# One PSUM ring for every use, and another order of the first pair's work, in a two-layer graph attention kernel

## The chip, the cores and the metric

The kernel runs on one core of a Trainium2 chip. The metric is device time in microseconds (us) of the whole launch. Lower is better. The engines are named as in the profile: PE is TensorE (PEld is its weight load), DVE is VectorE, ACT is ScalarE, POOL is GpSimd, and SP issues most DMAs.

## The reference, cut to what matters

Sixty-four graphs of 256 nodes with 512 features pass through two layers that share one 0/1 adjacency matrix:

```python
# layer 0: attention with 8 heads of 64, masked by adj
q, k, v = x @ Wq + bq, x @ Wk + bk, x @ Wv + bv
scores = q @ k.T / 8 + (1 - adj) * -1e9
x = layernorm(x + softmax(scores) @ v @ Wo + bo)
# layer 1: graph convolution
x = layernorm(x + (adj @ x) @ weight + bias)
```

All inputs and outputs are float32.

## The kernel before, in words

**Digits.** A plain float32 product is slow on PE, so most products are done in three products of float32r "digits". Each operand is cut into a high part, a low part and their scaled difference. The product then runs the three digit pairs (1, 0, 2) into one PSUM tile. Cutting one 128x512 operand costs ACT one or two operations and DVE two. For x it is `x_high` on ACT and `x_rest` on DVE (L262, L263). For a block of queries or keys, `product` first copies PSUM to a tile `uncut` on ACT (L329). Then `qk_high` (ACT, L334) and `qk_rest` (DVE, L341 and L343 or L345) cut it, and keys need a last scaling by ACT, `k_low` (L350). For weights it is `split_high` (ACT, L122) and `split_rest` (DVE L127, L128, then ACT L129).

**Weights.** Each of five weight sets (`v`, `qk0`, `qk1`, `o`, `l`) is cut once, in the ring tiles `wr` (six tiles, three to a set, so two sets at a time), and is kept in HBM by three 1 MB DMAs that SP issues (`keep`, L134). Later uses are loaded from there by POOL (`load_w`, L114) in the order of the list `STAGES`.

**Pairs.** Graphs are worked on two at a time: 32 pairs, `p` = 0 to 31. Heads come in two groups `g` = 0 and 1 of four heads. One pair's steps are: products of queries and keys of group 0, `scores(p, 0)`, the values' four blocks (`v`), queries and keys of group 1 (blocks 2 and 3), `values(p, 0)`, `scores(p, 1)`, and `values(p, 1)`, then the output product `o`, a layernorm, `adj_x`, the product `l` and a layernorm. `first(w)` and `second(w)` interleave the pair `w` with its neighbours w - 1 and w + 1. `start()` does the first pair and `last()` the last.

**Order.** On PE, DVE and ACT the instructions stand in the order in which the code lists them (`manual_schedule`). An engine that waits holds up everything listed after it on that engine. In `last()` that holds for PE alone. SP and POOL follow the scheduler's order.

**scores.** `scores(p, g)` (L393) makes eight PSUM tiles in four chunks of two. A chunk is 12 matmuls of 64x128 by 64x256. Two row halves of the array write two different tiles, and three digits of two heads go into each. ACT then takes the exponential of each tile into `e` (L409), DVE multiplies by the mask (`masked`, L414) and adds (`summed`, L419).

**values.** `values(p, g)` (L354) uses three tiles: the sums of the exponentials (L362, copied by ACT at L364), and one tile for each graph (L372, copied to `vc` by ACT at L376). DVE divides and writes `O` (L379 to L391).

**PSUM.** The eight banks are split into two rings. `ps_at` has five, for `scores` and `values`. `ps_mm` has three, for every `product`, `adj_x` (L491) and the transposes. A new tile takes the bank that was released longest ago in its ring, and its first matmul waits until the readers of that bank's last tile are done.

**The first pair.** Its weights are cut while it runs. Its first queries and keys (group 0) come from plain float32 products (`operands` returns one pair of operands) and are then cut into digits for `scores(0, 0)`. Its order in `start()` is: q, k of group 0; two `v` blocks; `scores(0, 0)`; two more `v` blocks; q, k of group 1; `values(0, 0)`; `scores(0, 1)`; then q, k of pair 1. The digits of `wo` are cut in `first(1)`, and those of the second layer's weight in `second(1)`, through their arguments `more[0]`, `more[1]` and `more[2]`.

Of the kernel before, what the change touches and what calls it, by code (L numbers as in the profile page):

```python
# [8 lines left out]
F32 = mybir.dt.float32  # L9
F32R = mybir.dt.float32r  # L10
I32 = mybir.dt.int32
AF = mybir.ActivationFunctionType
# [23 lines left out]
def fast(tc, x, adj, wq, bq, wk, bk, wv, bv, wo, bo, w1, b1, out):  # L36
# [27 lines left out]
    wring = pool("wr", 6)  # L64
    scratch = pool("scratch", 1, space=bass.MemoryType.DRAM)
    small = pool("small", 2)
    ps_at = pool("ps_at", 5, space=bass.MemoryType.PSUM)
    ps_mm = pool("ps_mm", 3, space=bass.MemoryType.PSUM)

    XC, XF, XP, R, Q, K, V, E, SM, O, SET, HL, ST, LN = ({} for _ in range(14))  # L70
    RAW, SCRATCH, W, UNCUT = {}, {}, {}, {}
# [25 lines left out]

    STAGES = [("v", 0), ("qk1", 0), ("qk0", 1)]  # L100
    for p in range(1, NP):
        STAGES += [("v", p), ("qk1", p), ("o", p - 1), *([("qk0", p + 1)] if p + 1 < NP else []), ("l", p - 1)]
    STAGES += [("o", NP - 1), ("l", NP - 1)]
# [99 lines left out]
    acc = cpool.tile([P, 2, N // 32], F32, name="acc")  # L203

    def adj_t():
        pt = ps_mm.tile([P, NC, N], F32, name="mm")
# [14 lines left out]
    def bv_wo():  # L221

        wide = one.tile([P, DC, P], F32, name="z")
        nc.vector.tensor_copy(wide, bv_s[:, :, None].to_broadcast([P, DC, P]))
        pm = ps_mm.tile([P, D], F32, name="mm")
        for d in range(DC):
            nc.tensor.matmul(pm, wide[:, d, :], RAW["o", d], start=d == 0, stop=d == DC - 1)
        nc.vector.tensor_tensor(bo_s, bo_s, pm, op=OP.add)
# [3 lines left out]
    def x_first(i):  # L232
        if i == 0:
            for d in range(DC):
                if d % 2 == 0:
                    t = one.tile([P, 2, D], F32, name=f"e{2 + d // 2}")
                XF[0, d] = t[:, d % 2]
        pt = ps_mm.tile([P, DC, P], F32, name="mm")
# [65 lines left out]
        return [pairs[i] for i in (1, 0, 2)]  # L304

    def product(name, p, j):
        pm = ps_mm.tile([P, D], F32, name="mm")
        pairs = [operands(name, p, j, k) for k in range(DC)]
        n = len(pairs[0])
        for i in range(n):  # L310
            for k in range(DC):
                nc.tensor.matmul(pm, *pairs[k][i], start=i == 0 and k == 0, stop=i == n - 1 and k == DC - 1)  # L312
        scale = RHO if n == 3 else 1.0
        b, c = divmod(j, 2)
        if name in "ol":
            r = R[p][b][:, c]
            if c == 0:
                ST[p, name, b] = two.tile([P, 2], F32, name="sums")
            nc.vector.scalar_tensor_tensor(r, pm, scale, r, op0=OP.mult, op1=OP.add, accum_out=ST[p, name, b][:, c:c + 1])  # L319
        elif name == "v":  # L320
            if c == 0:
                V[p, b] = two.tile([P, NC, D], F32, name="v")
            nc.scalar.activation(V[p, b][:, c], pm, AF.Copy, scale=scale)
        else:
            T, bias = (K, bk_s) if name == "k" else (Q, bq_s)
            if c == 0:
                T[p, b] = one.tile([P, 2, 3, D], F32R, name=name + "T")
            UNCUT[name, p, j] = two.tile([P, D], F32, name="uncut")
            nc.scalar.activation(UNCUT[name, p, j], pm, AF.Identity, bias=bias[:, j:j + 1], scale=scale)  # L329

    def qk_high(name, p, j):
        if 0 <= p < NP:
# [21 lines left out]
    def values(p, g, between=([], [])):  # L354
        if not 0 <= p < NP:
            do(*between)
            return
        at = ps_at.tile([P, 2, N], F32, name="at")
        for b in range(2):
            sm = SM.pop((p, g, b))  # L360
            for h in range(4):
# [2 lines left out]
        nc.scalar.activation(zc, at, AF.Copy)  # L364
        vc = []
        for b in range(2):
            at = ps_at.tile([P, 2, N], F32, name="at")
# [25 lines left out]
    def scores(p, g):  # L393
        if not 0 <= p < NP:
            return
        for b in range(2):
            for kc in range(NC):

                sc = [ps_at.tile([P, 2, N], F32, name="at") for s in range(2)]
                keys = slice(b * N + kc * P, b * N + (kc + 1) * P)  # L400
                for a in range(2):
                    for i in (1, 0, 2):
                        for s in range(2):
                            r = slice(s * HD, (s + 1) * HD)
                            nc.tensor.matmul(sc[s][:, a, :], K[p, g][r, a, i, keys], Q[p, g][r, a, i, b * N:(b + 1) * N],  # L405
                                             start=i == 1, stop=i == 2)
                e = E[p, g, b, kc] = one.tile([P, 2, 2, N], F32, name=f"e{2 * b + kc}")
                for s in range(2):
                    nc.scalar.activation(e[:, s], sc[s], AF.Exp, scale=RHO * qscale)  # L409

    def masked(p, g, b, kc):
        if 0 <= p < NP:
# [70 lines left out]
    def adj_x(p, b, half):  # L483

        if 0 <= p < NP:
            t = HL.pop((p, b, half))
            pm = ps_mm.tile([P, 2, N], F32, name="mm")
            for j in range(2):
                for mc in range(NC):
                    for i in range(2):  # L490
# [20 lines left out]
    def first(w, more=([], [], [])):  # L511
# [41 lines left out]

    def start():
        do(*((x_first, i) for i in range(4)), *((x_high, 0, i) for i in range(4)))
        v, qk1, qk0 = (pairs_of(ring_high, ring_rest, *stage) for stage in STAGES[:3])
# [17 lines left out]
        do((bv_wo,), (x_rest, 1, 2), (x_rest, 1, 3), (block, "q", 1, 0), masks(0, 1, 0), qk0[:2],  # L574
           (block, "k", 1, 0), qk0[2:4], (k_low, 1, 0), masks(0, 1, 1),
           (block, "q", 1, 1), qk0[4:6], (o_high, 0, 0, 0), (o_rest, 0, 0, 0),
           (block, "k", 1, 1), qk0[6:], (k_low, 1, 1), (stage_end, 0), (o_high, 0, 1, 0), (o_rest, 0, 1, 0))

    def last():

# [45 lines left out]
    count = ps_mm.tile([P, 1], F32, name="mm")  # L626
# [182 lines left out]
```

## Time and profile before

| what | us |
|---|---|
| median of 3 runs (2483.57 to 2483.84) | 2483.81 |
| the profiled execution, whole | 2484.97 |
| its span in the trace | 2483.2 |
| PE, PEld busy in the span | 2429.8, 1932.3 |
| DVE, ACT, POOL busy | 2012.2, 1506.9, 438.8 |
| one pair in the steady part (1209.65 to 1284.58 in the trace) | 74.93 |

The trace is of one execution. Times in it count from the start of its span, which is 1.77 us shorter than the same execution's whole time. PE's busy time is modelled from the instructions' sizes, so a PE that is shown busy may still wait a little between two matmuls. A bracket in a line of the timeline gives the idle time just before the group and what ended it.

### The profile page before, as it was taken

The numbers are of one execution on the slowest core, as the hardware profiler recorded it, in microseconds if no ns is written. First come the engines' busy times: TensorE is split into PE (matmuls) and PEld (weight loads), VectorE is DVE, ScalarE is ACT, GpSimd is POOL, SyncE is SP. The second block draws the span as 40 slices with busy tenths as digits, with TensorE's granted clock in tenths as the row PEclk, the third lists the DMA queues.
The fourth block names the chain that finished last, engine by engine and source line by source line (L and its number), as shares of the span: only waits on it lengthen the run. The fifth ranks groups of instructions, "written<-read, shape, count | busy, mean of one in ns | idle before, by whom it ended". The sixth has DMA issues, their size and how long they took to land.

```text
span 2483.2 us, 42881 instructions
## 1 busy us (share of the span) xinstructions
PE 2429.8 (98%) x16910; PEld 1932.3 (78%) x16910; DVE 2012.2 (81%) x3319; ACT 1506.9 (61%) x2802; POOL 438.8 (18%) x720
## 2 busy tenths in 40 slices
PE   8879999999999999999999999999999999999997
PEld 5657787787887787877887877877877877877876
DVE  6777889787889788888888888788888888888866
ACT  5556566666566566566565566566566666566554
POOL 0001111112111112112112112112122121122110
PEclk9989999999999999999999999999999999999998
DMA  7568877778777788777779777779778788778650
GB/s 244 176 212 271 273 238 227 266 250 272 259 239 235 258 252 285 250 237 239 255 248 299 248 226 247 248 253 303 240 224 256 249 255 290 239 226 267 243 187 36
DMA packets 370719, 603.45 MB, mean 243 GB/s; under 512 B 272848, under 2 KB 275152, under 8 KB 310224
## 3 DMA queue, kind: packets, MB, share of 16 engines
q0 software_dynamic: 65664, 478.18, 52.4%
q1 hardware_dynamic: 302736, 120.37, 21.2%
q8 instruction: 135, 2.21, 0.4%
q10 hardware_dynamic: 2112, 2.10, 0.2%
q14 instruction: 72, 0.59, 0.1%
HBM read 551.29 MB, written 49.28 MB: 242 GB/s over the span
## 4 chain that ended last, share of the span: by engine, by line
PE 90%; DVE 2%; ACT 1%; DMA 1%; issue 0%; POOL 0%; POOLq 0%; DVEq 0%; ACTq 0%; SPq 0%
PE mm L312 67%; PE at L405 9%; PE at L372 8%; PE mm L491 5%; PE at L362 2%; DMA r<-in_x_dram 0%; ACT r L464 0%; ACT waste L447 0%; DVE sl L262 0%; DVE wr L128 0%; DVE sd L263 0%; DVE e L414 0%; DVE r L428 0%; DVE r L319 0%; DVE hl L481 0%
## 5 line engine op out<-in xcount | busy, mean ns | idle before, releaser
L414 DVE TENSOR_TENSOR e<-e,adjT 128x1024 f32<-128x1024 f32 x256 | 304.7, 1222 | 1.2 <-ACT e L409 1.2
L312 PE MATMUL mm<-wr,sl 128*128 128x512 f32 x1024 | 279.5, 394 | 12.0 <-ACT wr L129 8.0
L312 PE MATMUL mm<-wr,sh 128*128 128x512 f32 x1024 | 276.3, 391 | 0.0
L312 PE MATMUL mm<-wr,sd 128*128 128x512 f32 x1024 | 275.2, 390 | 0.0
L312 PE MATMUL mm<-low,wr 128*128 128x512 f32 x992 | 273.0, 396 | 1.7 <-DVE low L262 1.7
L312 PE MATMUL mm<-high,wr 128*128 128x512 f32 x992 | 267.6, 391 | 0.0
L312 PE MATMUL mm<-diff,wr 128*128 128x512 f32 x992 | 265.9, 390 | 0.0
L409 ACT ACTIVATE e<-at 128x512 f32<-128x512 f32 x512 | 257.3, 627 | 8.7 <-PE at L405 8.5
L447 ACT ACTIVATE waste<-r,ln 128x512 bf16<-128x512 f32 x256 | 183.9, 718 | 110.8 <-DVE ln L440 108.7
L405 PEld LDWEIGHTS at<-qT,kT 64*128 64x128 f32 x3072 | 204.8, 188 | 57.9 <-issue 25.5
L405 PE MATMUL at<-qT,kT 64*128 64x256 f32 x3072 | 238.1, 294 | 11.5 <-ACT kT L350 7.3
L312 PEld LDWEIGHTS mm<-wr,sl 128*128 128x128 f32 x1024 | 191.0, 189 | 53.7 <-ACT wr L129 10.0
L372 PE MATMUL at<-e,v 128*32 128x256 f32 x4096 | 232.7, 379 | 0.0
L341 DVE SCALAR_TENSOR_TENSOR qT<-qT,uncut 128x512 fp32r<-128x512 f32 x128 | 87.9, 687 | 171.7 <-ACT qT L334 171.7
L464 ACT ACTIVATE r<-r,ln 128x512 f32<-128x512 f32 x256 | 194.1, 807 | 52.5 <-DMA x<-in_x_dram 27.1
L312 PEld LDWEIGHTS mm<-wr,sh 128*128 128x128 f32 x1024 | 193.8, 189 | 41.1
L453 POOL TENSOR_TENSOR ln<-ln,power 128x2 f32<-128x2 f32 x128 | 150.6, 1176 | 422.4 <-DVE ln L452 371.7
L312 PEld LDWEIGHTS mm<-wr,sd 128*128 128x128 f32 x1024 | 193.2, 189 | 40.6
L329 ACT ACTIVATE uncut<-mm,bq 128x512 f32<-128x512 f32 x128 | 88.1, 688 | 216.9 <-PE mm L312 165.5
L312 PEld LDWEIGHTS mm<-high,wr 128*128 128x128 f32 x992 | 186.8, 188 | 41.3
L312 PEld LDWEIGHTS mm<-diff,wr 128*128 128x128 f32 x992 | 186.8, 188 | 39.9
L312 PEld LDWEIGHTS mm<-low,wr 128*128 128x128 f32 x992 | 177.9, 188 | 38.2 <-DVE low L262 2.5
(104 smaller groups left out, 4216.7 us busy)
## 6 DMA issues: line engine op xcount, KB each, us to landing
wr<-qk POOLq DMA_DIRECT2D x183, 1024.0 KB, 7.3
wr<-v POOLq DMA_DIRECT2D x93, 1024.0 KB, 6.7
wr<-o POOLq DMA_DIRECT2D x90, 1024.0 KB, 8.2
wr<-l POOLq DMA_DIRECT2D x90, 1024.0 KB, 8.5
r<-in_x_dram SPq DMA_DIRECT2D x32, 1024.0 KB
x<-in_x_dram SPq DMA_DIRECT2D x496, 64.0 KB
out_dram<-r SPq DMA_DIRECT2D x62, 512.0 KB
qk<-wr SPq DMA_DIRECT2D x6, 1024.0 KB
```

What stands on the lines that cost most here:

```text
L312: nc.tensor.matmul(pm, *pairs[k][i], start=i == 0 and k == 0, stop=i == n - 1 and k == DC - 1)
L329: nc.scalar.activation(UNCUT[name, p, j], pm, AF.Identity, bias=bias[:, j:j + 1], scale=scale)
L341: nc.vector.scalar_tensor_tensor(low, high.bitcast(F32), -RHO, UNCUT.pop((name, p, j)), op0=OP.mult, op1=OP.add)
L362: nc.tensor.matmul(at[h * 32:(h + 1) * 32, b, :], ones, sm[:, h % 2, h // 2, :], start=True, stop=True)
L372: nc.tensor.matmul(at[h * 32:(h + 1) * 32, a, :], V[p, b][:, kc, col:col + 32], E[p, g, b, kc][:, h % 2, h // 2, :], start=kc == 0, stop=k ...
L405: nc.tensor.matmul(sc[s][:, a, :], K[p, g][r, a, i, keys], Q[p, g][r, a, i, b * N:(b + 1) * N], start=i == 1, stop=i == 2)
L409: nc.scalar.activation(e[:, s], sc[s], AF.Exp, scale=RHO * qscale)
L414: nc.vector.tensor_tensor(e, e, mask[:, kc:kc + 1, :].to_broadcast([P, 4, N]), op=OP.mult)
L447: nc.scalar.activation(waste, R[p][b][:, c], AF.Square, bias=t[0][:, c:c + 1], accum_out=t[1][:, c:c + 1])
L453: nc.gpsimd.tensor_tensor(t[2], t[1], power, op=OP.pow)
L464: nc.scalar.activation(r, r, AF.Identity, scale=t[2][:, c:c + 1], bias=t[3][:, c:c + 1])
L491: nc.tensor.matmul(pm[:, j, :], t[:, i, mc, j * P:(j + 1) * P], adjT[:, mc, :], start=mc == 0 and i == 0, stop=mc == NC - 1 and i == 1)
```

## The change

It has four parts. All PSUM tiles come from one ring of eight banks, in the order of their use. The first pair's first scores use one plain float32 matmul in place of three digits: ACT writes q and k of group 0 straight into `qT` and `kT`, with no cutting. In `start()` the first pair's queries and keys of group 1 come ahead of its `v` blocks, the weights' cutting follows that order (`STAGES` starts with `qk1`, then `v`), and some of the other steps are moved. In `first` the two `more` groups that hold half of `wo`'s cutting come right after the last `v` block, and the third comes before `qk_high` of the block after; `more` is empty for every pair but the second.

```diff
-    ps_at = pool("ps_at", 5, space=bass.MemoryType.PSUM)
-    ps_mm = pool("ps_mm", 3, space=bass.MemoryType.PSUM)
+    banks = pool("banks", 8, space=bass.MemoryType.PSUM)
...
-    STAGES = [("v", 0), ("qk1", 0), ("qk0", 1)]
+    STAGES = [("qk1", 0), ("v", 0), ("qk0", 1)]
...
     def product(name, p, j):
-        pm = ps_mm.tile([P, D], F32, name="mm")
+        pm = banks.tile([P, D], F32, name="ps")
...
             if c == 0:
-                T[p, b] = one.tile([P, 2, 3, D], F32R, name=name + "T")
-            UNCUT[name, p, j] = two.tile([P, D], F32, name="uncut")
-            nc.scalar.activation(UNCUT[name, p, j], pm, AF.Identity, bias=bias[:, j:j + 1], scale=scale)
+                T[p, b] = one.tile([P, 2, 3, D], F32R if n == 3 else F32, name=name + "T")
+            if n == 3:
+                to = UNCUT[name, p, j] = two.tile([P, D], F32, name="uncut")
+            else:
+                to = T[p, b][:, c, 0]
+            nc.scalar.activation(to, pm, AF.Identity, bias=bias[:, j:j + 1], scale=scale)
...
     def scores(p, g):
...
-                sc = [ps_at.tile([P, 2, N], F32, name="at") for s in range(2)]
+                sc = [banks.tile([P, 2, N], F32, name="ps") for s in range(2)]
...
-                    for i in (1, 0, 2):
+                    digits = (1, 0, 2) if (p, g) != (0, 0) else (0,)
+                    for i in digits:
...
-                                             start=i == 1, stop=i == 2)
+                                             start=i == digits[0], stop=i == digits[-1])
...
-           (block, "v", w, 2), (block, "v", w, 3), (stage_end, w), more[0],
-           (block, "q", w, 2), (qk_high, "q", w, 2), (qk_rest, "q", w, 2),
-           (block, "k", w, 2), (qk_high, "k", w, 2), (qk_rest, "k", w, 2), more[1],
-           (block, "q", w, 3), (k_low, w, 2), (qk_high, "q", w, 3), (qk_rest, "q", w, 3), more[2],
+           (block, "v", w, 2), (block, "v", w, 3), (stage_end, w), more[0], more[1],
+           (block, "q", w, 2), more[2], (qk_high, "q", w, 2), (qk_rest, "q", w, 2),
+           (block, "k", w, 2), (qk_high, "k", w, 2), (qk_rest, "k", w, 2),
+           (block, "q", w, 3), (k_low, w, 2), (qk_high, "q", w, 3), (qk_rest, "q", w, 3),
...
     def start():
...
-        do((block, "q", 0, 0), (qk_high, "q", 0, 0), (x_rest, 0, 0), (x_rest, 0, 1), v[0],
-           (block, "k", 0, 0), (qk_high, "k", 0, 0), (x_rest, 0, 2), (x_rest, 0, 3), v[1],
-           (block, "q", 0, 1), (qk_high, "q", 0, 1), v[2], (block, "k", 0, 1), (qk_high, "k", 0, 1), (adj_t,),
-           (qk_rest, "k", 0, 0), (k_low, 0, 0), (qk_rest, "q", 0, 0), (qk_rest, "k", 0, 1), (k_low, 0, 1), (qk_rest, "q", 0, 1),
-           qk1[0], (block, "v", 0, 0), qk1[1], (block, "v", 0, 1))
+        do((block, "q", 0, 0), (x_rest, 0, 0), (x_rest, 0, 1), qk1[0], (block, "k", 0, 0), (x_rest, 0, 2), (x_rest, 0, 3), qk1[1],
+           (block, "q", 0, 1), qk1[2], v[0], (block, "k", 0, 1), (square_adj,), (adj_t,))
         scores(0, 0)
-        do(qk1[2], (square_adj,), masks(0, 0, 0), (x_t, 1, 0), (x_t, 1, 1),
-           (block, "v", 0, 2), (x_high, 1, 0), (x_high, 1, 1), masks(0, 0, 1),
-           (block, "v", 0, 3), (stage_end, 0), (x_rest, 1, 0), (x_rest, 1, 1), (x_t, 1, 2), (x_t, 1, 3),
-           (block, "q", 0, 2), (qk_high, "q", 0, 2), qk0[0],
-           (block, "k", 0, 2), (qk_high, "k", 0, 2), (qk_rest, "q", 0, 2), (qk_rest, "k", 0, 2), (k_low, 0, 2), qk0[1],
-           (block, "q", 0, 3), (qk_high, "q", 0, 3), (x_high, 1, 2), (x_high, 1, 3), qk0[2],
-           (block, "k", 0, 3), (qk_high, "k", 0, 3), (qk_rest, "q", 0, 3), (qk_rest, "k", 0, 3), (k_low, 0, 3),
-           (stage_end, 0), (load_r, 0), (load_l,))
+        do(v[1], masks(0, 0, 0), (block, "q", 0, 2), v[2], (qk_high, "q", 0, 2), (qk_rest, "q", 0, 2), (x_t, 1, 0), (x_t, 1, 1),
+           (block, "k", 0, 2), (x_high, 1, 0), (x_high, 1, 1), (qk_high, "k", 0, 2), (qk_rest, "k", 0, 2), masks(0, 0, 1),
+           (block, "q", 0, 3), (k_low, 0, 2), (qk_high, "q", 0, 3), (qk_rest, "q", 0, 3), (x_rest, 1, 0), (x_t, 1, 2),
+           (block, "k", 0, 3), (stage_end, 0), (qk_high, "k", 0, 3), (qk_rest, "k", 0, 3), (x_rest, 1, 1), (x_t, 1, 3), qk0[0],
+           (block, "v", 0, 0), (k_low, 0, 3), (x_high, 1, 2), (x_rest, 1, 2), (block, "v", 0, 1), qk0[1],
+           (block, "v", 0, 2), (x_high, 1, 3), (x_rest, 1, 3), qk0[2], (block, "v", 0, 3), (stage_end, 0), (load_r, 0), (load_l,))
         values(0, 0)
         scores(0, 1)
...
-        do((bv_wo,), (x_rest, 1, 2), (x_rest, 1, 3), (block, "q", 1, 0), masks(0, 1, 0), qk0[:2],
+        do((bv_wo,), (block, "q", 1, 0), masks(0, 1, 0), qk0[:2], (block, "k", 1, 0), qk0[2:4], masks(0, 1, 1),
...
```

`pairs_of` returns a weight set's cutting in three parts: [0] is the high parts of two operands, [1] is one rest, one high, one rest, one high, and [2] is the last two rests. The other uses of the two old pools (transposes, `bv_wo`, `values`, `adj_x`) take `banks` too.

More of the change, by code (lines that the diff above doesn't have):

```diff
@@ L205, in adj_t @@
     def adj_t():
-        pt = ps_mm.tile([P, NC, N], F32, name="mm")
+        pt = banks.tile([P, NC, N], F32, name="ps")
         for mc in range(NC):
@@ L237, in x_first @@
                 XF[0, d] = t[:, d % 2]
-        pt = ps_mm.tile([P, DC, P], F32, name="mm")
+        pt = banks.tile([P, DC, P], F32, name="ps")
         for d in range(DC):
@@ L306, in product @@
     def product(name, p, j):
-        pm = ps_mm.tile([P, D], F32, name="mm")
+        pm = banks.tile([P, D], F32, name="ps")
         pairs = [operands(name, p, j, k) for k in range(DC)]
@@ L357, in values @@
             return
-        at = ps_at.tile([P, 2, N], F32, name="at")
+        at = banks.tile([P, 2, N], F32, name="ps")
         for b in range(2):
@@ L366, in values @@
         for b in range(2):
-            at = ps_at.tile([P, 2, N], F32, name="at")
+            at = banks.tile([P, 2, N], F32, name="ps")
             for a in range(2):
@@ L405, in scores @@
                             nc.tensor.matmul(sc[s][:, a, :], K[p, g][r, a, i, keys], Q[p, g][r, a, i, b * N:(b + 1) * N],
-                                             start=i == 1, stop=i == 2)
+                                             start=i == digits[0], stop=i == digits[-1])
                 e = E[p, g, b, kc] = one.tile([P, 2, 2, N], F32, name=f"e{2 * b + kc}")
                 for s in range(2):
-                    nc.scalar.activation(e[:, s], sc[s], AF.Exp, scale=RHO * qscale)
+                    nc.scalar.activation(e[:, s], sc[s], AF.Exp, scale=(RHO if (p, g) != (0, 0) else 1.0) * qscale)
     def masked(p, g, b, kc):
@@ L486, in adj_x @@
             t = HL.pop((p, b, half))
-            pm = ps_mm.tile([P, 2, N], F32, name="mm")
+            pm = banks.tile([P, 2, N], F32, name="ps")
             for j in range(2):
@@ L555, in start @@
         do(*((x_first, i) for i in range(4)), *((x_high, 0, i) for i in range(4)))
-        v, qk1, qk0 = (pairs_of(ring_high, ring_rest, *stage) for stage in STAGES[:3])
-        do((block, "q", 0, 0), (qk_high, "q", 0, 0), (x_rest, 0, 0), (x_rest, 0, 1), v[0],
-           (block, "k", 0, 0), (qk_high, "k", 0, 0), (x_rest, 0, 2), (x_rest, 0, 3), v[1],
-           (block, "q", 0, 1), (qk_high, "q", 0, 1), v[2], (block, "k", 0, 1), (qk_high, "k", 0, 1), (adj_t,),
-           (qk_rest, "k", 0, 0), (k_low, 0, 0), (qk_rest, "q", 0, 0), (qk_rest, "k", 0, 1), (k_low, 0, 1), (qk_rest, "q", 0, 1),
-           qk1[0], (block, "v", 0, 0), qk1[1], (block, "v", 0, 1))
@@ L562, in start @@
-        scores(0, 0)
-        do(qk1[2], (square_adj,), masks(0, 0, 0), (x_t, 1, 0), (x_t, 1, 1),
-           (block, "v", 0, 2), (x_high, 1, 0), (x_high, 1, 1), masks(0, 0, 1),
-           (block, "v", 0, 3), (stage_end, 0), (x_rest, 1, 0), (x_rest, 1, 1), (x_t, 1, 2), (x_t, 1, 3),
-           (block, "q", 0, 2), (qk_high, "q", 0, 2), qk0[0],
-           (block, "k", 0, 2), (qk_high, "k", 0, 2), (qk_rest, "q", 0, 2), (qk_rest, "k", 0, 2), (k_low, 0, 2), qk0[1],
-           (block, "q", 0, 3), (qk_high, "q", 0, 3), (x_high, 1, 2), (x_high, 1, 3), qk0[2],
-           (block, "k", 0, 3), (qk_high, "k", 0, 3), (qk_rest, "q", 0, 3), (qk_rest, "k", 0, 3), (k_low, 0, 3),
-           (stage_end, 0), (load_r, 0), (load_l,))
+        qk1, v, qk0 = (pairs_of(ring_high, ring_rest, *stage) for stage in STAGES[:3])
@@ L573, in start @@
         qk0 = [(f, name, 1, j) for j in range(2) for name in "qk" for f in (qk_high, qk_rest)]
-        do((bv_wo,), (x_rest, 1, 2), (x_rest, 1, 3), (block, "q", 1, 0), masks(0, 1, 0), qk0[:2],
-           (block, "k", 1, 0), qk0[2:4], (k_low, 1, 0), masks(0, 1, 1),
-           (block, "q", 1, 1), qk0[4:6], (o_high, 0, 0, 0), (o_rest, 0, 0, 0),
-           (block, "k", 1, 1), qk0[6:], (k_low, 1, 1), (stage_end, 0), (o_high, 0, 1, 0), (o_rest, 0, 1, 0))
+        do((bv_wo,), (block, "q", 1, 0), masks(0, 1, 0), qk0[:2], (block, "k", 1, 0), qk0[2:4], masks(0, 1, 1),
+           (block, "q", 1, 1), (k_low, 1, 0), qk0[4:6], (o_high, 0, 0, 0), (o_high, 0, 1, 0), (o_rest, 0, 0, 0),
+           (block, "k", 1, 1), qk0[6:], (stage_end, 0), (k_low, 1, 1), (o_rest, 0, 1, 0))
     def last():
@@ L625, in fast @@
     nc.vector.tensor_reduce(least, good, AX.XY, OP.min)
-    count = ps_mm.tile([P, 1], F32, name="mm")
+    count = banks.tile([P, 1], F32, name="ps")
     nc.tensor.matmul(count[0:32], ones, least, start=True, stop=True)
```

## The prediction

> **What bounds the kernel now.** I began with the page's busy times and slices.
>
> ```profile
> PE 2429.8 (98%) x16910; PEld 1932.3 (78%) x16910; DVE 2012.2 (81%) x3319; ACT 1506.9 (61%) x2802; POOL 438.8 (18%) x720
> ...
> PE   8879999999999999999999999999999999999997
> ```
>
> PE is the bound, and its visible idle time lies in the first four slices (248 us) and the last. So I looked inside the full stretch, at one `scores` of the timeline, PE and then PEld.
>
> ```profile
> 1243.60 3.69 PE L405 MATMUL at<-qT,kT 64*128 64x256 f32 x48
> 1247.22 0.50 PE L312 MATMUL mm<-wr,low 128*128 128x512 f32 x1
> ...
> 1243.60 2.52 PEld L405 LDWEIGHTS at<-qT,kT 64*128 64x128 f32 x37 [0.41 <-issue]
> 1246.32 0.77 PEld L405 LDWEIGHTS at<-qT,kT 64*128 64x128 f32 x11 [0.20 <-ACT e L409]
> ```
>
> This stage lasts 3.62 us (1247.22 - 1243.60), and its fourth chunk waits for ACT's exponential. The waits of 300 to 2300 us show that this repeats:
>
> ```profile
> PEld at L405 <- ACT e L409: 11.2, 55, 0.3
> ```
>
> The starts of single matmuls in the trace give the size. Pairs of matmuls (two row halves, 3 ns apart) follow every 0.120 us, but the 13th pair comes 0.088 us late and the 19th 0.156 us late, and the pair after each comes 0.10 us late too. That is 0.088 + 0.102 + 0.156 + 0.103 = **0.45 us**. In the other half of a pair's work (`second`, 1209.65 to 1213.20) it is 0.012 + 0.102 + 0.163 + 0.103 = **0.38 us**. With a ring of five, chunk 3 needs the banks of `values`' last tile and of the first `scores` tile, and chunk 4 those of the next two `scores` tiles, whose exponentials ACT has just begun. No other place of the steady part waits: the same steps take the same 74.93 us each time.
>
> Then PE's waits of the first 180 us:
>
> ```profile
> 69.84 1.01 PE L405 MATMUL at<-qT,kT 64*128 64x256 f32 x6 [7.34 <-ACT kT L350]
> 131.66 0.79 PE L312 MATMUL mm<-wr,sl 128*128 128x512 f32 x1 [5.07 <-ACT wr L129]
> 167.62 1.21 PE L491 MATMUL mm<-adjT,hl 128*128 128x256 f32 x8 [2.87 <-ACT uncut L329]
> 176.71 1.65 PE L491 MATMUL mm<-adjT,hl 128*128 128x256 f32 x6 [4.86 <-ACT uncut L329]
> ```
>
> The first waits for keys whose cutting DVE reached late, the second for `wo`'s digits, the last two for a bank of the ring of three.
>
> **What the Trainium skill says.** "Perfetto Trace Analysis", Identifying the Most-Contended Engine, says that matmul busy time is no measure of the distance to the limit; its Optimization Strategy says that a gap that keeps repeating can mean too little PSUM for the next tile. The trace agrees: PE reads 2000 of 2000 us busy and repeats two gaps in each `scores`. "TensorE: Matmul & The Clock Gate", What's actually happening, says that the array runs at half clock after about 3.4 us of idleness. The trace agrees: after 5.07 us matmuls came every 0.427 us instead of 0.227 for 6 us, after 2.87 us not at all. "FP8 and Floating Point Precision", TensorE Precision Notes, gives true FP32 four passes. Here a plain 128x512 matmul takes 0.86 us (two records of 0.43) against 0.227, 3.8 times.
>
> **The change, part by part.**
>
> *Ring, steady part.* With eight banks in turn, the built order gives chunk 3 the banks of the sums (copied by ACT before the stage begins) and of the last product (L319, ended 1.7 us before), and chunk 4 those of `values`' two tiles. The last `vc` copy ends 1.2 us (first half) or 0.74 us (second) after the stage begins. Chunk 4 needs it at 2.4 us. So both waits go. The product after takes the bank of the first `scores` tile, whose exponential ends at 1.1 + 0.5 = 1.6 us, and is due at 3.17. Every later tile has as long or longer. Per pair 0.45 + 0.38 = 0.83 us. From where the start leaves off (`scores(2, 0)`): 30 x 0.45 + 29 x 0.38 = **24.5 us**. DVE (83% busy there) and ACT (62%) have room for 1% less time.
>
> *Start, up to `scores(1, 0)` (98.21 before).* Removed: 8 DVE operations of 0.69 (5.5 us), 4 `qk_high` and 2 `k_low` on ACT (3.7 us). PE: 48 digit matmuls (4.24 us there) become 16 plain ones. No plain one of 64x256 is in the trace; in overlapping row halves it is 8 x 0.43 = 3.4 us, without overlap 6.9. I take 3.4; the difference lies ahead of a wait of PE that is longer. I laid the listed order out with the trace's own spacings (DVE cutting 1.33 a pair of operations, masks of one graph 3.5, `x_t` 0.65; ACT 0.5 to 0.6). Plain q and k end at 25.8 as now, `scores(0, 0)` runs 26.3 to 30, q and k of group 1 to 41, `v` to 52. DVE, busy from 27.0, has 4 weight operands (5.3), masks (7.1), 4 `qk_rest` (5.3), 4 `x_t` (2.6), 4 `x_rest` (5.3) and 4 `qk0` operands (5.3): 31 us, and about 5 us of waits for ACT, so it ends at 62.9. The fourth `v` copy stands behind the last two L129 on ACT, so it ends at 64.1. `values(0, 0)` needs it: PE waits 9.4 us from 54.6 and restarts at half clock. That is the new stall in place of the 7.3 us. `scores(0, 1)` then runs 67.1 to 71.2 (before: ended at 74.7), `bv_wo` to 74.7. Then q(1, 0) goes without the waits on `low` and the half clock that made it last until 84.86: it ends at 77.4. Three blocks, a 0.8 us wait for the masks and 4.1 us of `values` bring `scores(1, 0)` to 90.6: **7.6 us** gained. On SP, `qk1`'s three keeps now precede `v`'s. SP issues until 32.5 anyway (`bv`, `bo`), and pair 1's `x` loads of 39 us meet both sets' 6 MB; in the trace such loads took 7.5 to 9.5 us, and `x_t` needs them at 48.5, which is just in time (bound: 0 to 2 us late). POOL's next load, v(1), is due only at 93.8.
>
> *`wo`'s digits.* DVE is free of masks and `with_bo` 17.5 us after `scores(1, 0)` begins. Four rests of 1.33 and the last L129 end at 23.6; the first `o` block is due at 25.1. So the 6.2 us of waits and about 4 us of half clock go. But q and k of blocks 2 and 3 are copied and cut later (by about 5 us), and DVE reaches `values(1, 0)`'s transposition at 42.2 us after `scores(1, 0)` (before 51.5; in the steady part 40.0). Gain **9.3 us**.
>
> *`l`'s digits in `second(1)`.* Order unchanged. The bank waits (2.87 and 4.86 us) go, but DVE and ACT go on as before: from DVE's transposition at 149.75 to the last L129 at 176.1 is 26.35 us, and the first `l` block then starts at once, not at 178.38. Gain 2.3, and 0.4 of half clock: **2.7 us**. PE now waits about 5 us for the digits instead.
>
> *End.* `o` of pair 31 loses a bank wait (1.63 us at 2398), and `scores(31, 1)` its waits. I cost both at nothing: DVE sat 6.7 us for pair 31's `r` (DMA), and what follows hangs on DVE and ACT, whose orders are unchanged (bounds 0 to 2 us).
>
> **Sum.** 24.5 + 7.6 + 9.3 + 2.7 = 44.1 us off the profiled execution's 2484.97 (span 2483.2) gives 2440.9. That execution stands 1.16 us above the median, so **2439.7 us**.
>
> **The rivals.**
> *Start stalls again* (0.14): `wo`'s digits or the `v` copies come 5 us later than laid out, and each stall past 3.4 us costs half clock too. For it: DVE and ACT wait for each other through `k_low`, and the margin at `o` is 1.5 us. The start then gives 8 instead of 19.6: 2451.
> *The gaps in `scores` are not the banks'* (0.06), but the change of operands or ACT's pace: only the start gains, 2464. Against it: no gap at chunk 2, whose banks are free.
> *The change does not do what it says* (0.02): banks go out by release, not by age, `scores` still meets late ones, and the start moves nothing; 2484. Against it: the order as built, where chunk 4 has `values`' two banks in every pair.
> *Slower* (0.03): in one ring the product after `scores` waits for that stage's first exponential. It has 1.6 us to spare. If ACT began 2.6 us later than now, 1 us would be lost in 62 stages, 62 - 44 = +18: 2502. It decides from 1.6 + 44/62 = 2.3 us. Against it: L409 begins 1.0 to 1.1 us after the stage in both halves, and nothing on ACT moves there.
>
> **Numbers.** The forecast has 0.75, own range 2432 to 2447: below, PE alone bounds the start (7 us more); above, the `x` loads and half clock. With the stalling start the range reaches 2453. A measurement here tells 0.2% (5 us) from no change. Faster by more 0.95, within 0.02, slower 0.03.
>
> **What would show it.** Right: `scores` lasts 3.17 us, a pair 74.1; PE's waits on L409 are gone; waits near 55 to 64 us (on L323) and about 5 us before the first `l` block, none before `o`. Wrong: a pair of 74.9, or a wait of PE on L129 after 100 us.

## The result, and the profile after

The changed kernel takes 2448.03 us (median of 4 runs: 2439.61, 2447.75, 2448.30, 2450.93) against 2483.69 for the kernel before. The ratio is 0.9852, 95% interval 0.9827 to 0.9876: 35.7 us less. The forecast was 2439.7, with a range of 2432 to 2447 of its own, which its rival of a stalling start widened to 2453. The time is 8.3 us above the forecast: 1 us outside the first range and inside the wider one. Its runs lie 11 us apart, those of the kernel before 1 us (3.6 and 5.9 us in the two later sets that were taken beside the experiments).

The profiled execution took 2448.3 us with a span of 2446.5, 36.7 less than before. The starts of four `scores` stages cut both spans into stretches (us):

| stretch | before | after | gain | forecast |
|---|---|---|---|---|
| span's start to `scores(1, 0)` | 98.21 | 103.88 | -5.7 | +7.6 |
| `scores(1, 0)` to `scores(2, 0)` | 96.58 | 84.13 | +12.4 | +12.0 (9.3 + 2.7) |
| `scores(2, 0)` to `scores(31, 1)` | 2215.10 | 2181.59 | +33.5 | +24.5 |
| `scores(31, 1)` to the end | 73.32 | 76.86 | -3.5 | 0 |

So the sum, 44.1 us, came within 7.4 us of the measured 36.7, but three of its four terms were off by 13.3, 9.0 and 3.5 us, and not all the same way. The busy times and slices of the page after hardly show any of it:

```profile
PE 2391.2 (98%) x16894; PEld 1915.0 (78%) x16894; DVE 2004.2 (82%) x3311; ACT 1503.7 (61%) x2796; POOL 439.8 (18%) x720
...
PE   8789999999999999999999999999999999999987
```

PE is the bound as before. Its second slice fell from 8 to 7 (61 to 122 us, where the new start stalls) and its third rose from 7 to 8 (where `wo`'s digits had been late).

**Steady part.** One `scores` in the timeline, PE and then PEld (start, busy time, engine, line, tiles, count):

```profile
1222.01 3.14 PE L408 MATMUL ps<-qT,kT 64*128 64x256 f32 x48
1225.08 1.19 PE L311 MATMUL ps<-wr,low 128*128 128x512 f32 x4
...
1222.01 2.93 PEld L408 LDWEIGHTS ps<-qT,kT 64*128 64x128 f32 x48 [0.41 <-PE ps L374]
```

All 48 weight loads are one group now, and no bracket names ACT's exponential. The stage lasts 3.07 us from start to start (1225.08 - 1222.01), in the other half of a pair too. A pair takes 73.81 us instead of 74.93.

**Start.** PE's timeline ahead of `scores(0, 1)`, DVE's two transposes of pair 1's last `x` tiles, ACT, and POOL's load of the `v` weights:

```profile
56.67 1.50 PE L374 MATMUL ps<-e,v 128*32 128x256 f32 x24 [2.65 <-ACT v L322]
71.57 1.08 PE L374 MATMUL ps<-e,v 128*32 128x256 f32 x8 [13.39 <-ACT v L322]
77.34 2.79 PE L374 MATMUL ps<-e,v 128*32 128x256 f32 x24 [4.70 <-ACT v L322]
```

```profile
52.95 0.71 DVE L250 STREAM_TRANSPOSE xT<-x 128x512 f32<-128x512 f32 x1 [3.78 <-DMA x<-in_x_dram]
...
65.11 0.71 DVE L250 STREAM_TRANSPOSE xT<-x 128x512 f32<-128x512 f32 x1 [8.83 <-DMA x<-in_x_dram]
```

```profile
68.56 0.63 ACT L128 ACTIVATE wr<-wr 128x512 fp32r<-128x512 f32 x1 [11.94 <-DVE wr L127]
...
70.94 0.58 ACT L322 ACTIVATE v<-ps 128x512 f32<-128x512 f32 x1
```

```profile
51.34 1.26 POOL L113 DMA_DIRECT2D wr<-v  x2 [49.95 <-PE ps L311]
```

Read from the end: PE waits 20.7 us for three copies of `v`. On ACT these copies stand behind `L128`, which waits 11.94 us for DVE's weight digits. DVE had stood still until 65.11 for the fourth `x` tile of pair 1. That tile was still on its way when POOL issued its 3 MB of loads, from 51.34 on. DVE's two waits, 12.6 us, are what the forecast had put at 0 to 2.

**`l`'s digits.** PE, just before the first `l` block:

```profile
170.31 0.80 PE L311 MATMUL ps<-wr,sl 128*128 128x512 f32 x1 [3.12 <-ACT wr L128]
171.64 0.80 PE L311 MATMUL ps<-wr,sl 128*128 128x512 f32 x1 [0.53 <-ACT wr L128]
```

**Tail.** DVE waits for pair 31's `r`, and then PE (timeline):

```profile
2355.31 2.36 DVE L431 TENSOR_TENSOR r<-r,bo 128x1024 f32<-128x1024 f32 x2 [6.30 <-DMA r<-in_x_dram]
```

```profile
2372.59 0.38 PE L408 MATMUL ps<-qT,kT 64*128 64x256 f32 x1 [0.57 <-ACT vc L378]
2375.33 0.97 PE L408 MATMUL ps<-qT,kT 64*128 64x256 f32 x11 [2.37 <-ACT vc L378]
2376.52 3.63 PE L494 MATMUL ps<-adjT,hl 128*128 128x256 f32 x16 [0.21 <-ACT e L412]
2382.39 0.73 PE L311 MATMUL ps<-wr,sl 128*128 128x512 f32 x2 [2.24 <-DVE sl L261]
2384.20 1.22 PE L311 MATMUL ps<-wr,sl 128*128 128x512 f32 x2 [1.07 <-DVE sl L261]
2385.22 1.91 PE L311 MATMUL ps<-wr,sh 128*128 128x512 f32 x4
```

The 16 matmuls of `adj_x` take 3.63 us where other groups of 16 take 2.05, and groups of four in a product take 1.91 where they take 1.07: half clock. The trace's record of the granted clock shows it twice here, from 2376.4 to 2379.8 and from 2383.3 to 2390.1 us. The first stretch stands in the kernel before too (2415.9 to 2419.3, after waits of 0.46, 1.77 and 0.81 us with matmuls between them; `adj_x` took 2.71). The second does not. PE at the same place before:

```profile
2421.25 0.73 PE L312 MATMUL mm<-wr,sl 128*128 128x512 f32 x2 [0.61 <-DVE sl L262]
2423.05 0.73 PE L312 MATMUL mm<-wr,sl 128*128 128x512 f32 x2 [1.07 <-DVE sl L262]
2423.62 1.09 PE L312 MATMUL mm<-wr,sh 128*128 128x512 f32 x4
```

These matmuls wait for `sl`, the digits that DVE makes, and start 27.08 us after DVE begins `with_bo` (L431; L428 before) in both kernels (2382.39 - 2355.31 and 2421.25 - 2394.17). In the changed kernel PE is there earlier, and so waits longer.

### The profile page after: what moved, and what is told of

It reads as the page before. It is cut to its first block, busy times and chain, and to the rows that moved or that the text cites. A ratio compares the mean times of both kernels' runs of the same rounds, so it can differ in the third digit from the quotient of the medians.

```text
span 2446.5 us, 42891 instructions
## 1 busy us (share of the span) xinstructions
PE 2391.2 (98%) x16894; PEld 1915.0 (78%) x16894; DVE 2004.2 (82%) x3311; ACT 1503.7 (61%) x2796; POOL 439.8 (18%) x720
## 4 chain that ended last, share of the span: by engine, by line
PE 89%; DVE 3%; ACT 1%; DMA 1%; issue 0%; POOL 0%; POOLq 0%; SPq 0%; DVEq 0%; ACTq 0%
PE ps L311 67%; PE ps L374 8%; PE ps L408 7%; PE ps L494 5%; PE ps L364 2%; DMA r<-in_x_dram 1%; ACT r L467 0%; DMA o<-wr 0%; ACT waste L450 0%; DVE sl L261 0%; DVE e L417 0%; DVE sd L262 0%; DVE r L318 0%; DVE r L431 0%; DVE hl L484 0%; DVE wr L127 0%
## 5 line engine op out<-in xcount | busy, mean ns | idle before, releaser
L311 PE MATMUL ps<-wr,sl 128*128 128x512 f32 x1024 | 277.6, 392 | 7.0 <-ACT wr L128 3.6
L311 PE MATMUL ps<-wr,sh 128*128 128x512 f32 x1024 | 276.0, 391 | 0.0
L311 PE MATMUL ps<-wr,sd 128*128 128x512 f32 x1024 | 275.2, 390 | 0.0
L311 PE MATMUL ps<-low,wr 128*128 128x512 f32 x992 | 271.5, 395 | 0.0
L311 PE MATMUL ps<-high,wr 128*128 128x512 f32 x992 | 266.5, 390 | 0.0
L311 PE MATMUL ps<-diff,wr 128*128 128x512 f32 x992 | 265.0, 389 | 0.0
L412 ACT ACTIVATE e<-ps 128x512 f32<-128x512 f32 x512 | 257.0, 627 | 10.0 <-PE ps L408 9.8
L374 PE MATMUL ps<-e,v 128*32 128x256 f32 x4096 | 235.1, 381 | 20.7 <-ACT v L322 20.7
L311 PEld LDWEIGHTS ps<-wr,sh 128*128 128x128 f32 x1024 | 193.4, 189 | 41.0
L408 PE MATMUL ps<-qT,kT 64*128 64x256 f32 x3056 | 204.2, 286 | 3.8 <-ACT vc L378 3.8
```

What stands on the lines that cost most here:

```text
L412: nc.scalar.activation(e[:, s], sc[s], AF.Exp, scale=(RHO if (p, g) != (0, 0) else 1.0) * qscale)
```

## The experiments

Each line of this table is one kernel. The stretches are those above, from its profile; the second is divided at `scores(1, 1)`. The ratios are to runs of the kernel before made beside each experiment (medians 2483.36 for e1 to e4 and 2483.95 for e5 to e8). Each stretch comes from one execution. Kernels whose order is the same there still differ: by 3.4 us up to `scores(1, 0)` (e1 and e2), by 1.6 from `scores(1, 1)` to `scores(2, 0)` (changed, e4 to e8), by 2.3 at the end (changed, e1, e2, e4 to e6), by 0.8 in the steady part. Line numbers in a kernel's profile shift by a few with its edits, so the tiles are named too.

| kernel | median us | ratio to before, 95% | to (1,0) | (1,0) to (1,1) | (1,1) to (2,0) | (2,0) to (31,1) | to the end |
|---|---|---|---|---|---|---|---|
| before | 2483.69 | 1 | 98.21 | 52.54 | 44.04 | 2215.10 | 73.32 |
| changed | 2448.03 | 0.9852 (0.9827 to 0.9876) | 103.88 | 40.66 | 43.47 | 2181.59 | 76.86 |
| e1 ring alone | 2449.19 | 0.9865 (0.9849 to 0.9882) | 95.11 | 50.60 | 41.77 | 2181.36 | 77.47 |
| e2 ring, `wo` | 2442.49 | 0.9834 (0.9818 to 0.9851) | 98.47 | 40.86 | 44.65 | 2181.51 | 76.94 |
| e3 changed, banks split | 2475.43 | 0.9975 (0.9962 to 0.9989) | 94.90 | 41.78 | 45.15 | 2214.97 | 73.24 |
| e4 early `x` | 2435.94 | 0.9812 (0.9796 to 0.9829) | 91.23 | 40.66 | 44.89 | 2180.97 | 75.44 |
| e5 held load | 2436.03 | 0.9812 (0.9798 to 0.9825) | 94.84 | 40.65 | 43.56 | 2181.52 | 77.58 |
| e6 e4 with digits | 2442.20 | 0.9835 (0.9820 to 0.9850) | 98.50 | 40.66 | 44.41 | 2181.00 | 75.24 |
| e7 e4, `with_bo` placed | 2430.97 | 0.9791 (0.9776 to 0.9806) | 90.97 | 40.65 | 43.31 | 2181.76 | 72.34 |
| e8 e7, `v` first | 2428.81 | 0.9777 (0.9762 to 0.9792) | 89.13 | 40.66 | 43.32 | 2181.72 | 72.15 |

The theory: the banks give the whole steady gain. The new start would gain too, but loses it to late `x` tiles. The tail turns PE's saved time into idleness and half clock.

**e1: the ring alone.**

```diff
 # the kernel before
-    ps_at = pool("ps_at", 5, space=bass.MemoryType.PSUM)
-    ps_mm = pool("ps_mm", 3, space=bass.MemoryType.PSUM)
+    banks = pool("banks", 8, space=bass.MemoryType.PSUM)
```

> The kernel before with its PSUM pools alone replaced by one ring of eight banks; no order is changed and the first scores keep their digits. If the steady gain is all the banks' (the theory): `scores` lasts 3.07 us in both halves, a pair 73.8 us, scores(2,0) to scores(31,1) shrinks by 33 us as in the changed kernel, the tail gives back about 3.5 us by half clock, the wait for wo's digits stays: 2450 to 2454 us. If the order had a part in it (the rival): a pair stays above 74.2 us and the time above 2460.

Measured 2449.19, 0.8 us below the expected range. PE's timeline in the steady part:

```profile
1221.26 3.14 PE L404 MATMUL ps<-qT,kT 64*128 64x256 f32 x48
1224.33 1.19 PE L311 MATMUL ps<-wr,low 128*128 128x512 f32 x4
```

`scores` again lasts 3.07 us and a pair 73.81, and the steady part shrinks by 33.7 us. The tail loses 4.1. So the ring alone does all of the steady gain, and it alone brings the loss in the tail. It comes within 1.2 us of the whole change.

**e2: ring and `wo`'s digits.**

```diff
 # e1, in first()
-           (block, "v", w, 2), (block, "v", w, 3), (stage_end, w), more[0],
-           (block, "q", w, 2), (qk_high, "q", w, 2), (qk_rest, "q", w, 2),
-           (block, "k", w, 2), (qk_high, "k", w, 2), (qk_rest, "k", w, 2), more[1],
-           (block, "q", w, 3), (k_low, w, 2), (qk_high, "q", w, 3), (qk_rest, "q", w, 3), more[2],
+           (block, "v", w, 2), (block, "v", w, 3), (stage_end, w), more[0], more[1],
+           (block, "q", w, 2), more[2], (qk_high, "q", w, 2), (qk_rest, "q", w, 2),
+           (block, "k", w, 2), (qk_high, "k", w, 2), (qk_rest, "k", w, 2),
+           (block, "q", w, 3), (k_low, w, 2), (qk_high, "q", w, 3), (qk_rest, "q", w, 3),
```

> The ring of eight and the new place of wo's digits in first(1), with the start of the kernel before (values ahead of queries and keys, digits in the first scores). Theory: no wait of PE before the first `o` block, scores(1,0) to scores(1,1) takes 41 to 43 us instead of 52.5, so 10 to 12 us below e1, about 2441; that is below the changed kernel, because the new start lost time. Rival (the stretch is shorter only because the new start left DVE and ACT less behind): scores(1,0) to scores(1,1) stays above 46 us and the kernel within 5 us of e1.

The stretch to `scores(1, 1)` is 9.7 us shorter than in e1, close to what was expected. But the next is 2.9 longer, so the order alone gives 6.9 us in these two stretches and 6.7 in the medians, not 10 to 12. (The two profiled executions differ by 3.9 us as a whole, as e2's first stretch is 3.4 us longer than e1's with the same code.) The 2.9 us are not a longer wait for `l`'s digits, which fell from 3.12 + 0.53 to 1.93 + 0.54 us. PE has run ahead of ACT and DVE: it loses 2.1 us in `scores(1, 1)`, where it waits for copies of `vc`, and 1.0 us at the last `adj_x` ahead of `l`, where it waits for `hl`. With the old start this kernel is 5.5 us below the changed one in the medians.

**e3: the banks split again.**

```diff
 # the changed kernel
-    banks = pool("banks", 8, space=bass.MemoryType.PSUM)
+    ps_at = pool("ps_at", 5, space=bass.MemoryType.PSUM)
+    ps_mm = pool("ps_mm", 3, space=bass.MemoryType.PSUM)
```

> The changed kernel with the old split of five and three banks; everything else as changed. Theory: `scores` goes back to 3.55 and 3.62 us and a pair to 74.93, the start and wo's part as in the changed kernel or a few us worse (waits for a bank of the ring of three), the tail about 3.5 us better: 2476 to 2484 us. Rival (the new order of the start is worth time by itself, and the ring less): below 2470.

Measured 2475.43 over 8 runs, 0.6 us below the expected range. `scores` in the timeline, PE and then PEld, and the product after it:

```profile
1230.28 3.69 PE L409 MATMUL at<-qT,kT 64*128 64x256 f32 x48
1233.90 1.21 PE L312 MATMUL mm<-wr,low 128*128 128x512 f32 x4
...
1230.28 2.52 PEld L409 LDWEIGHTS at<-qT,kT 64*128 64x128 f32 x37 [0.41 <-issue]
1232.99 0.77 PEld L409 LDWEIGHTS at<-qT,kT 64*128 64x128 f32 x11 [0.20 <-ACT e L413]
```

The wait for the exponential is back (3.62 us from start to start), the steady part is that of the kernel before, and the tail too (73.24). The runs fall into two groups: four at 2471.5 to 2472.7 and four at 2478.2 to 2482.6, and the median stands between them. It is 7.9 us below the kernel before, so the new order is worth something without the ring, but much less than the ring. In the profiled execution DVE waits 3.29 us for the third `x` tile and not at all for the fourth, and `scores(1, 0)` starts at 94.90, 9 us earlier than in the changed kernel's profile.

**e4: early `x` tiles.**

```diff
 # the changed kernel, load_x(), the loads at the start, and x_t()
-            t = XC[p, i] = two.tile([P, D], F32, name="x")
+            early = p == 1 and i > 1
+            t = two.tile([P, D], F32, name="o" if early else "x")
+            XC[p, i] = t
...
-    for i in range(2):
+    for i in range(4):
         load_x(1, i)
...
-            load_x(p + k // 2, (k + 2) % DC)
+            if (p, k // 2) != (1, 0):
+                load_x(p + k // 2, (k + 2) % DC)
```

> The changed kernel with the third and fourth x tile of pair 1 loaded at the very start, into the two `o` tiles that nothing uses yet, and so ahead of the six 1 MB keeps on SP's queue. Theory (DVE's waits of 3.8 and 8.8 us for these loads hold up the weights' cutting, the copies of `v` behind it on ACT and so PE): these waits go, PE's wait on L322 before values(0,0) falls from 20.7 us to 8 to 11 us, scores(1,0) starts near 91 instead of 103.9 us, 2434 to 2438 us in all, and the runs spread less than 2439.6 to 2450.9. Rival (ACT's own queue or the weights' digits hold the copies anyway): scores(1,0) stays within 3 us of 103.9 and the time within 3 us of 2448.

Measured 2435.94, runs 2434.18 to 2437.61. DVE waits for no `x` tile. PE ahead of `scores(0, 1)`:

```profile
59.24 1.03 PE L377 MATMUL ps<-e,v 128*32 128x256 f32 x8 [3.48 <-ACT v L325]
65.02 2.79 PE L377 MATMUL ps<-e,v 128*32 128x256 f32 x24 [4.74 <-ACT v L325]
67.73 3.94 PE L411 MATMUL ps<-qT,kT 64*128 64x256 f32 x48
```

The last copy of `v` ends at 64.96, `scores(0, 1)` starts at 67.73 and `scores(1, 0)` at 91.23. The prediction had 64.1, 67.1 and 90.6. So its layout of the start was right but for the tiles' arrival.

**e5: POOL's load held.**

```diff
 # the changed kernel, x_t()
             nc.vector.transpose(XF[p, k], XC.pop((p, k)))
+            if (p, k) == (1, 3):
+                held = small.tile([P, 16], F32, name="seen")
+                nc.gpsimd.tensor_tensor(held, XF[p, k][:, 0:16], XF[p, k][:, 0:16], op=OP.add)
```

> The changed kernel with one tiny POOL operation on the transposed fourth x tile of pair 1 put ahead of POOL's 3 MB load of the v weights, so that this load cannot start before the tile is in. Theory (the fourth tile's small packets lose against this load: landed 65.1 us with the load issued at 51.3 us; in e3's profile, where the tile landed in time, scores(1,0) started at 94.9): DVE never waits 8.8 us for it, scores(1,0) starts at 94 to 96 us, and all runs lie at 2438 to 2441 us, where only one of four of the changed kernel did. Rival (the six keeps ahead on SP's queue are what delays the tile): the wait of 8.8 us stays, and the time stays at 2448 in most runs.

```profile
52.63 0.71 DVE L250 STREAM_TRANSPOSE xT<-x 128x512 f32<-128x512 f32 x1 [2.75 <-DMA x<-in_x_dram]
...
55.89 0.70 DVE L250 STREAM_TRANSPOSE xT<-x 128x512 f32<-128x512 f32 x1
```

```profile
57.27 1.80 POOL L113 DMA_DIRECT2D wr<-v  x3
```

The fourth tile is transposed at 55.89, with no wait, instead of 65.11, and only then does the load start. Nothing on SP's queue was changed, and the keeps ahead of the tiles are all there. So the 8.8 us were POOL's load. What the keeps may account for is the third tile's wait: it lasts 2.75 us here, 3.78 in the changed kernel and 3.29 in e3, and nothing in e4; in the traces the first small packet of the two tiles moves only at 49.1 us (here) and 49.6 us (changed), after the keeps' packets on the same queue. The transfers of 49.5 to 52 us in the changed kernel, before POOL's load moves anything, and then of 57 to 61 us (queue, packets, MB, share of the 16 engines):

```profile
q1 hardware_dynamic: 2626, 0.48, 98.6%
...
q0 software_dynamic: 206, 1.55, 99.7%
q1 hardware_dynamic: 205, 0.03, 35.6%
```

POOL's queue (q0) moves 7.5 KB a packet, the `x` tiles' queue (q1) 0.13 KB. The Trainium skill ("DMA: Bandwidth & Descriptors", Queues, rings and completion order) says that each DMA engine takes turns between its queues packet by packet. The trace agrees: 206 packets against 205, one for one, and so in each single us (43 and 41, 49 and 50, 65 and 64, 49 and 50). So the `x` tiles go from 1050 packets a us to 51. `scores(1, 0)` starts at 94.84, as expected. The median, 2436.03, is 2 us below what I expected. Three runs are at 2435.6 to 2436.0, the other two at 2439.9 (profiled) and 2441.7. What sets these two groups apart isn't settled; the third tile's wait of 2.75 us in the profiled one is a candidate.

**e6: digits in the first scores.**

```diff
 # e4; q and k of group 0 go to `uncut` again, and the exponential has the scale of digits
-                    digits = (1, 0, 2) if (p, g) != (0, 0) else (0,)
+                    digits = (1, 0, 2)
...
-        do((block, "q", 0, 0), (x_rest, 0, 0), (x_rest, 0, 1), qk1[0], (block, "k", 0, 0), (x_rest, 0, 2), (x_rest, 0, 3), qk1[1],
-           (block, "q", 0, 1), qk1[2], v[0], (block, "k", 0, 1), (square_adj,), (adj_t,))
+        do((block, "q", 0, 0), (qk_high, "q", 0, 0), (x_rest, 0, 0), (x_rest, 0, 1), qk1[0],
+           (block, "k", 0, 0), (qk_high, "k", 0, 0), (x_rest, 0, 2), (x_rest, 0, 3), qk1[1], (qk_rest, "k", 0, 0), (k_low, 0, 0), (qk_rest, "q", 0, 0),
+           (block, "q", 0, 1), (qk_high, "q", 0, 1), (block, "k", 0, 1), (qk_high, "k", 0, 1), (qk_rest, "k", 0, 1), (k_low, 0, 1), (qk_rest, "q", 0, 1),
+           qk1[2], v[0], (square_adj,), (adj_t,))
```

> e4 (early x tiles) with the first pair's first scores in digits again: 8 more DVE operations, 4 qk_high and 2 k_low ahead of scores(0,0). Theory (the stretch to values(0,0) hangs on DVE's sum of work, 0.69 us an operation): everything up to the fourth v copy comes 5 to 6 us later, scores(1,0) at 96 to 97 us, 2440 to 2442 us. Rival (DVE and ACT have slack there and plain scores bring nothing): within 2 us of e4's 2435.9.

Measured 2442.20, with `scores(1, 0)` at 98.50, that is 7.3 us later than in e4 (5 to 6 were expected; the medians differ by 6.3). So plain scores are what the new start gains. With digits, queries and keys ahead of values start `scores(1, 0)` no earlier than the old order in e1 and e2 (95.11 and 98.47), even with early `x` tiles. I placed the digits' steps myself; another place could be better.

**e7: `with_bo` of pair 31 placed by hand.**

```diff
 # e4, first(), behind the second o block (and no longer in last())
            (block, "o", q, 1), (mean, q, "o", 0), (squared, q, "o", 0), (squared, q, "o", 1),
+           *([(with_bo, w, b) for b in range(2)] if w == NP - 1 else []),
```

> e4 with the bias addition of pair 31 (with_bo, DVE L431 in the changed kernel) listed by hand behind the second o block of first(31); the scheduler had put it ahead of two operations on keys, where DVE waited 6.3 us for pair 31's r. Theory (the tail hangs on this wait, and PE's 3.5 us that the ring saves there turn into idle time and half clock): the wait and PE's waits in scores(31,1) go, no half clock after it, scores(31,1) to the end takes 68 to 72 us instead of 75.4, 2430 to 2433 us. Rival (the tail is bound by DVE and ACT work behind scores(31,1)): within 1.5 us of e4.

Measured 2430.97. DVE and PE in the tail:

```profile
2347.74 2.36 DVE L434 TENSOR_TENSOR r<-r,bo 128x1024 f32<-128x1024 f32 x2
```

```profile
2356.68 3.52 PE L411 MATMUL ps<-qT,kT 64*128 64x256 f32 x48
2360.42 2.10 PE L497 MATMUL ps<-adjT,hl 128*128 128x256 f32 x16 [0.21 <-ACT e L415]
2366.30 1.02 PE L314 MATMUL ps<-wr,sl 128*128 128x512 f32 x2 [3.78 <-DVE sl L264]
```

DVE no longer waits for `r`, and PE no longer inside `scores(31, 1)`. The tail is 3.1 us shorter in the profile: 72.34, just above the 68 to 72 expected. The rest of the 5.0 us in the medians lies in stretches that e7 does not change. Half clock isn't gone: it now follows the 3.78 us that PE waits for DVE's digits of `adj_x`'s result.

**e8: `v` copies first.**

```diff
 # e7, start()
-           (block, "v", 0, 0), (k_low, 0, 3), (x_high, 1, 2), (x_rest, 1, 2), (block, "v", 0, 1), qk0[1],
-           (block, "v", 0, 2), (x_high, 1, 3), (x_rest, 1, 3), qk0[2], (block, "v", 0, 3), (stage_end, 0), (load_r, 0), (load_l,))
+           (block, "v", 0, 0), (k_low, 0, 3), (x_high, 1, 2), (x_rest, 1, 2), (block, "v", 0, 1),
+           (block, "v", 0, 2), (x_high, 1, 3), (x_rest, 1, 3), (block, "v", 0, 3), (stage_end, 0), qk0[1], (load_r, 0), (load_l,))
         values(0, 0)
+        do(qk0[2])
```

> e7 with the last two thirds of qk0's cutting behind the first pair's v blocks instead of between them, so that the third and fourth v copy on ACT no longer stand behind the scalings that wait for DVE. Theory: PE's two waits on L322 (3.5 and 4.7 us) and the half clock after them go, at the price of a wait of 0 to 3 us for qk0's digits before q(1,0): scores(1,0) at 83 to 87 us, 4 to 8 us below e7. Rival (the digits are as late as the copies were, so that the same wait moves to q(1,0)): scores(1,0) stays at 90 to 92 us.

```profile
68.11 5.11 PE L228 MATMUL ps<-hl,z 128*128 128x512 f32 x8 [5.12 <-ACT e L415]
```

PE waits for no copy of `v`, but now 5.12 us for an exponential of `scores(0, 1)`, which stands on ACT behind the last third of `qk0`'s cutting. `scores(1, 0)` starts at 89.13, 1.8 us earlier (2.2 in the medians, where 4 to 8 were expected): nearer the rival than the theory. At 2428.81 (2428.51 to 2428.91) it is the fastest kernel of this study, 19.2 us below the changed one.

## Why the prediction was right, and where two errors met

**Total.** It was right to 8.3 us, 1 us outside the range of the forecast proper, and that it came so close is luck. In the profile errors cancel: the steady part gave 9.0 us more than the sum, the start 13.3 less, the tail 3.5 less.

**Ring, steady part: mechanism right, size off.** Both waits went, as laid out from the banks' order, and e1 and e3 show the banks to be the whole cause. The mis-sized term was 0.83 us a pair: `scores` gave 0.480 and 0.552 instead of 0.38 and 0.45. In the starts of single matmuls before, the two row halves of the 13th pair stand 0.128 us apart in one half of the work and 0.205 in the other, instead of 0.003. I booked that as 0.012 and 0.088 of delay. In fact the first row half ran on its own, in the slot of a pair, and so did the second at the end: 24 pairs took 25 slots, and 0.10 us more was lost than I counted. A 3.17 us `scores` became 3.07. Over the 59 stages of this stretch `scores` gave 30.0 us, 5.5 more than the 24.5. Another 1.6 us is the bank wait of pair 31's `o`, which lies in this stretch and which the prediction had put at nothing, under its end. The other 1.9 us are small gains inside the products, 0.06 us a pair: "No other place of the steady part waits" was not quite so.

**Start: the failed step is "0 to 2 us late".** The removal of DVE's work was right: e6 prices the plain scores at 7.3 us up to `scores(1, 0)`. Plain scores lasted 3.65 us (I took 3.4 and not 6.9). The layout was right within 0.9 us, as e4 shows. But pair 1's third and fourth `x` tiles came 3.8 and 8.8 us late. The prediction named POOL's next load and dismissed it as "due only at 93.8". That asked when the load is needed, not when it is issued. That load goes into the weight tiles that the first pair's last block reads. In the changed order this is a `v` block, which ends at 52.6 us; before it was a block of keys, which ended at 57.5. So the load is issued from 51.34 on, 5 us earlier than before. In the kernel before, the last `x` tile had just landed (DVE, then POOL):

```profile
55.87 0.71 DVE L251 STREAM_TRANSPOSE xT<-x 128x512 f32<-128x512 f32 x1 [1.73 <-DMA x<-in_x_dram]
...
56.23 1.26 POOL L114 DMA_DIRECT2D wr<-v  x2 [54.85 <-DMA x<-in_x_dram]
```

(The end of POOL's wait is put down to `x` here, but that is inferred: in e1 the tile had landed by 55.11, and the load was issued at 55.79 all the same.) Which comes first decides, and e5 and e4 settle it. The two groups of e3 and the run of 2439.61 of the changed kernel would fit a tile that now and then wins it; of those runs only the profiled ones show the tile.

**`wo`'s and `l`'s digits.** The sum of both, 12.0, met 12.4. The split is different. Of the stretches up to `scores(2, 0)`, e1 takes 92.37 us against 96.58: the ring alone gives 4.2 (1.9 ahead of `scores(1, 1)`, 2.3 after it). e2 then gives 9.7 ahead of it and loses 2.9 after it. So `wo`'s 9.3 and `l`'s 2.7 each have about their size when taken alone, but the second does not outlast the first. PE's waits for `l`'s digits were 3.12 + 0.53 us, a little less than the 5 named, and none was left before `o`. (The first `l` block began at 178.59 before the change; the prediction reads 178.38.)

**End: "I cost both at nothing (bounds 0 to 2)" failed with the sign.** The reason was right: the tail hangs on DVE, which waits for `r` (6.73 us before, 6.30 after). From the end of that wait PE reached `scores(31, 1)` 15.7 us later before, 14.3 after. So PE gained 1.4 us there, about the bank wait of `o`, and had to wait it out: `sl` came after the same 27.08 us, and PE's wait for it grew from 0.61 to 2.24 us. Then came the half clock that the kernel before does not have here: from the second pair of `sl` matmuls to the next `adj_x` PE took 7.9 us instead of 5.1. A later stretch of half clock was 0.6 us cheaper. From DVE's `with_bo` to the end is 89.0 us before and 91.2 after, which is 2.2 more. The prediction used the clock rule of the Trainium skill ("TensorE: Matmul & The Clock Gate", What's actually happening: half clock after about 3.4 us of idleness) for the start and not for the tail. Here less was enough: no wait was longer than 2.24 us in the 3.41 us ahead of that half clock. A gain ahead of a fixed wait can cost more than nothing.

**Rivals.** "Start stalls again" gave 2451, 3.0 us from the measured time and nearer than the forecast. Its first two stretches gained 6.8 us together, where it said 8. The `v` copies did come late, but through DMA and not through DVE and ACT waiting for each other. "The gaps in `scores` are not the banks'" fell with e1. "The change does nothing" and "slower" fell with the times: in the steady part of the changed kernel the product after `scores` never waits for the first exponential.

## What to carry to other kernels

When an order of work is changed, ask of each queue when its next transfer is *issued*, not only when it is due: a buffer that comes free earlier starts a large load earlier, and a small transfer of tiny packets beside it can come 9 us late. One ring for all PSUM tiles was worth 34 us here without any change of order, so try it alone first. Where the end of a kernel hangs on one late transfer, time saved ahead of it turns into idleness and half clock; look for what waits behind that transfer.

## What was not expected of the hardware

- Two row halves that lose step cost a slot. Paired matmuls of 64x256 start every 0.120 us, both halves within 0.003. In the kernel before, one half starts alone in the 13th pair, the other 0.13 or 0.21 us later, and a stage of 24 pairs takes 25 slots. That costs 0.10 us on top of the late starts.
- Small packets starve beside large ones. The fourth `x` tile (4 x 64 KB in packets of 0.13 KB) was transposed at 65.1 us with a 3 MB load issued at 51.3, and at 55.9 with that load held back. While both moved, the two queues' packets went one for one (205 and 206 in 4 us).
- Half clock does not need one long wait. In all ten traces the granted clock changes only at steps of 3.41 us (2376.43, 2379.84, 2383.25 and 2390.08 us in the changed kernel's tail). From 20 us to the last products, a step at full clock in which PE was idle for 2.0 us or more, in one piece or several, was always followed by half clock, and one with up to 1.4 us never; between these both occurred. PE was idle for 2.4 us of the step up to 2383.25. The single wait of 2.87 us that ended at 167.62 in the kernel before brought no half clock: it fell into two steps, with 1.7 and 1.2 us of idleness. (Idleness by the modelled ends of the matmuls.)
- Plain float32 matmuls of 64x256 in two row halves overlap: 32 records in 3.65 us, a pair of records every 0.216 us.
